# Where the writes of split queries and keys are issued in a two-layer cross-attention kernel

## The chip, the core and the metric

The kernel is written for Trainium2 and runs on one core of one chip. A core has a matrix engine (TensorE, PE in the profile; its weight loads are listed apart as PEld), VectorE (DVE), ScalarE (ACT), GpSimd (POOL) and SyncE (SP), each with an instruction queue of its own that it works through in order. Transfers (DMAs) are issued from the queues of SP, ACT or GpSimd. The metric is the device time of one execution in microseconds. The kernel before takes 3375.44 us, the median of three runs (3371.98 to 3381.5).

## What is computed

Two layers, each of self attention, cross attention against a context of 1601 rows, and a gated feed-forward block, all in 32-bit floats. There are 4 batch elements, 512 positions, width 320, 20 heads of 16, and a hidden width of 1280:

```python
def _attn(x, ctx, wq, wk, wv, wo, bo, heads):
    ...
    q = (x @ wq).reshape(b, n, heads, dh).transpose(0, 2, 1, 3)
    k = (ctx @ wk).reshape(b, j, heads, dh).transpose(0, 2, 1, 3)
    v = (ctx @ wv).reshape(b, j, heads, dh).transpose(0, 2, 1, 3)
    sim = jnp.einsum('bhid,bhjd->bhij', q, k) * scale
    a = jax.nn.softmax(sim, axis=-1)
    out = jnp.einsum('bhij,bhjd->bhid', a, v)
    ...
    return out @ wo + bo
h1 = _ln(x, n1_g, n1_b)
x = _attn(h1, h1, q1, k1, v1, o1_w, o1_b, heads) + x
h2 = _ln(x, n2_g, n2_b)
x = _attn(h2, context, q2, k2, v2, o2_w, o2_b, heads) + x
h3 = _ln(x, n3_g, n3_b)
proj = h3 @ ff_w1 + ff_b1
a, g = jnp.split(proj, 2, axis=-1)
ff = a * jax.nn.gelu(g, approximate=False) @ ff_w2 + ff_b2
return ff + x
```

## The kernel before

Work is cut into units. A unit of attention is one batch element and one group of four heads, so a stage of attention has 4 x 5 = 20 units; a unit of feed-forward is one batch element. In order there are, for each layer, 20 units of self attention, 20 of cross attention and 4 of feed-forward. A unit of attention goes through its keys in chunks of 128 (4 chunks in self attention, 13 in cross attention). The main loop (`main`, from line 1154) does one chunk in two half rounds; the planner's clock (`clock["round"]`) counts half rounds, so a self unit has 8 and a cross unit 26.

In a chunk TensorE forms the scores `st` (L1165): the four heads each use 32 rows of the matrix engine, two products of queries and keys and a third that subtracts the row's maximum, held in `nrows`. ScalarE takes the exponential into `pr` (L1175). TensorE multiplies it with the values into `av` (L1189), ScalarE copies that to `vo` (L1205), and GpSimd adds it onto the unit's output `o` (L1206). `pr` and `vo` share one pool of nine buffers. Beside this, in the same half rounds, TensorE forms the scores `sps` of the next unit (L972), from which VectorE takes the row maxima (L989). At a unit's end these are split, turned and sent to `nrows` by four small transfers (`max_end`, L1050), before the next unit's third products can run.

Queries and keys are held as two parts, high (rounded) and low (the rest), so that a head of 16 fills 32 rows. A projection makes them some units ahead: `both` (L765) for self attention, where queries and keys of one group of heads come in two parts, and `keys_of_context` (L831) and `queries` (L802) for cross attention. ScalarE writes the product to `low` (L781, L810; the keys of context go to `stages` by L840 and L841), then GpSimd splits it: a rounded copy to `high` (L684), and a subtraction that leaves the rest in `low` (L685). `low` and `high` have one buffer each. To bring the parts into the rows that TensorE needs, they are written to `q_way` or `k_way` in DRAM and read back to `q` and `kT` (all at L729). Each of the two ways has two buffers, taken in turn.

These transfers are queued by `move` as entries of `u.moves`, a list for each unit for queries and one for keys. After each step `carry` (L666) issues what is at the head of the lists: an entry may go two half rounds after the one before it in its list (or after the projection), and a call stops once three or more transfers have gone. All go to SP's queue but those of the first unit. A unit has two entries of writes and one of reads. `pending` counts writes not yet issued; a new projection may start when there are none and the reads two users back have been issued (`way_free`). A unit's queries and keys may be used three half rounds after its last reads were issued (`at_hand`, L1401). `at_once` issues at once what a unit that is due still lacks.

When a unit ends, its `o` is divided by the row sums on VectorE and written to `oway` by SP (L1080). After the last group of heads an errand, two half rounds later, reads the batch element's outputs back as `aT` (L1089), and three half rounds after that the output projection (`project`, L1099) may begin, in eight pieces spread between the chunks.

The choice of what runs beside the chunks is made when the program is built: chains of work with a cost and a due time each (`add`, `pick`, `steps`), so the order on every engine is fixed.

Of the kernel before, what the change touches and what calls it, by code (L numbers as in the profile page):

```python
# [65 lines left out]
def kernel(ctx: ExitStack, tc: tile.TileContext, x, context, ws, out):  # L66
# [595 lines left out]
    errands = deque()  # L662
    pending = {"q": 0, "k": 0}
    movers = []

    def carry():  # L666

        room = 3
        for _, what, u in sorted(movers):
            todo = u.moves[what]  # L670
            while todo and todo[0][1]() and clock["round"] >= u.moving[what] + 2 and room > 0:
                room -= todo[0][2]
                todo.popleft()[0]()
            if not todo:
                movers.remove((u.i, what, u))
        while errands and room > 0 and clock["round"] >= errands[0][0] and errands[0][1]():
            errands.popleft()[2]()
# [9 lines left out]
    def add_proj(u):  # L687
# [32 lines left out]

        def move(of, n, pairs, may=None):

            def f():
                if may is None:
                    pending[of] -= 1
                u.moving[of] = clock["round"]
                for i, (to, src) in enumerate(pairs()):
                    queue = (nc.sync, nc.scalar, nc.gpsimd)[i % 3] if start["on"] and u.i == 0 else nc.sync
                    queue.dma_start(out=to, in_=src)  # L729
                if may is not None:  # L730
                    u.open -= 1
                    if not u.open:
                        u.when = -9 if start["on"] else clock["round"]

            if may is None:
                pending[of] += 1
            u.moves[of].append((f, may or yes, n))
            u.moving[of] = clock["round"]
            if (u.i, of, u) not in movers:
                movers.append((u.i, of, u))  # L740

# [5 lines left out]
        def way_free(what):  # L747

            return not pending[what] and (len(users[what]) < 2 or not any(users[what][-2].moves.values()))

        def read_queries(t, keys=None):
# [4 lines left out]

            move("q", 2 if keys is None else 3, pairs, lambda: unread() and (u.cross or free()))

        def both(part):
# [27 lines left out]
            to_q = on_way("q")  # L787
            move("q", 2, lambda: [(to_k[:, 0], high[GD:]), (to_k[:, 1], low[GD:])])
            move("q", 3, lambda: [(to_q[:, e], t[:GD]) for e, t in enumerate((high, low, high))])
            read_queries(to_q, to_k)  # L790
# [4 lines left out]
        def queries():  # L795
# [17 lines left out]
            for i in range(2):  # L813
                rows = slice(i * GD, (i + 1) * GD)
                cols = slice(i * w, (i + 1) * w)
                lo, hi = (t[rows, :w] for t in (low, high))
                pairs = [(to_q[:, e, :, cols], t) for e, t in enumerate((hi, lo, hi))]
                move("q", 3, lambda pairs=pairs: pairs)
            read_queries(to_q)
# [3 lines left out]
        def keys_of_context():  # L823
# [21 lines left out]
            for i in range(2):  # L845
                rows = slice(i * GD, (i + 1) * GD)
                pairs = [(to_k[:, h, :, i], t[rows].rearrange("p a w -> p (a w)")) for h, t in enumerate((high, low))]
                move("k", 2, lambda pairs=pairs: pairs)
            of = to_k.rearrange("j h d i (a w) -> (j h d) i a w", a=4)
# [6 lines left out]

            move("k", 3, reads, free)
            first.made["kv"] += 1
# [193 lines left out]
    def add_finish(u):  # L1052
# [24 lines left out]
        def turn():  # L1077
# [13 lines left out]

            errands.append((clock["round"] + 2, lambda: held["open"] < 2, read))

# [14 lines left out]
        def end(aT):  # L1108
            now = clock["round"]
            held["open"] += 1  # L1110
            for t in range(NQ):
                for part in range(2):
                    add(
                        "project", (0.317,) * 3, lambda t=t, part=part: project(aT, t, part),
                        now + 6 + u.nch * t + u.nch // 2 * part, yes, lambda: clock["round"] >= now + 3,
                    )
# [284 lines left out]
    def at_hand(v):  # L1401

        return v.when is not None and clock["round"] >= v.when + 3

# [159 lines left out]
```

## Time and profile before

| | |
|---|---|
| median of three runs | 3375.44 us |
| the profiled execution | 3384.97 us |
| its span, first to last instruction | 3383.2 us |
| mean granted TensorE clock | 0.946 of full speed |
| ScalarE busy with the exponentials (L1175) | 1407.0 us, 2720 instructions |
| GpSimd busy with the additions onto `o` (L1206) | 741.6 us, 576 instructions |
| transfers | 244.14 MB in 209045 packets |
| of these on SP's and ACT's queue (q1) | 238.02 MB |
| on GpSimd's (q0) | 0.40 MB, three transfers at the start |

A row of the waits reads: who waited (engine, tile, line), who ended the wait, microseconds in all, number of times, the longest. A row of the timeline has the start and the length in microseconds, then the engine (with a q for its queue's own instructions), the line, the operation, out<-in, and in square brackets how long the engine was idle before it and who ended that. A row of the windows has a stretch and its length, then busy microseconds and instructions of each engine, the granted clock, the share of DMA time and GB/s. A row of a group ends with busy microseconds, mean nanoseconds of one, and the idle time before.

### The profile page before, as it was taken

To read this page: it belongs to the slowest core of one execution; us is meant where nothing else is said; L and a number is where in the kernel's file an instruction comes from. 1 tells how busy PE (TensorE), PEld (TensorE's weight loads), DVE (VectorE), ACT (ScalarE), POOL (GpSimd) and SP (SyncE) were. 2 spreads that over 40 slices of the span, in tenths; PEclk is the share of its full clock that TensorE was granted. 3 is DMA by queue.
4 is the path that set the end of the run, shared out by engine and by line. 5 is a ranking of instruction groups with operands and counts; after the bars stand their busy time and mean duration, and the time that the engine had idled before them with its cause. 6 is when DMAs were issued, how large, how long until landed. Compare 5 with 4: busy or idle time off the path is not lost.

```text
span 3383.2 us, 81116 instructions
## 1 busy us (share of the span) xinstructions
PE 3121.4 (92%) x34290; PEld 1649.8 (49%) x34290; DVE 2096.4 (62%) x2819; ACT 1965.6 (58%) x3909; POOL 1130.3 (33%) x1224
## 2 busy tenths in 40 slices
PE   6889889999989989999999888899999899899999
PEld 3445445445545545445554554454454454454555
DVE  3657776767866876732237777667677677675221
ACT  1555656677767777830116665567677677686110
POOL 2333323443434443410113332234344344343000
PEclk7888999999989999999999999899999899999999
DMA  3343322222222222110023332222222122122000
GB/s 90 107 128 123 104 70 80 82 90 63 74 82 64 89 75 64 50 57 1 18 62 120 117 104 88 83 67 72 72 77 77 51 87 72 51 66 77 8 8 16
DMA packets 209045, 244.14 MB, mean 72 GB/s; under 512 B 60412, under 2 KB 140424, under 8 KB 208680
## 3 DMA queue, kind: packets, MB, share of 16 engines
q1 hardware_dynamic: 207924, 238.02, 22.7%
q8 instruction: 269, 4.41, 0.5%
q14 instruction: 96, 0.79, 0.1%
q10 hardware_dynamic: 308, 0.53, 0.1%
q0 software_dynamic: 448, 0.40, 0.0%
HBM read 130.03 MB, written 107.55 MB: 70 GB/s over the span
## 4 chain that ended last, share of the span: by engine, by line
PE 61%; DMA 17%; DVE 8%; SPq 5%; issue 3%; ACT 3%; POOL 1%; ACTq 0%; POOLq 0%; DVEq 0%
PE st L1165 16%; PE av L1189 13%; PE fps L1295 8%; PE yps L1349 5%; DMA q<-qway 4%; DMA qway<-low 4%; DVE pm L989 4%; DMA qway<-high 3%; PE kps L831 3%; SPq L729 3%; PE sps L972 3%; PE ops L1099 3%; ACT pr L1175 2%; DMA aT<-oway 2%; PE fps L1308 2%
## 5 line engine op out<-in xcount | busy, mean ns | idle before, releaser
L1175 ACT ACTIVATE pr<-st 128x512 f32<-128x512 f32 (+1 forms) x2720 | 1407.0, 602 | 449.5 <-PE st L1165 391.0
L989 DVE TENSOR_REDUCE pm<-sps 128x2 f32<-128x1024 f32 (+1 forms) x975 | 1135.5, 1200 | 228.3 <-PE sps L972 192.7
L1206 POOL TENSOR_TENSOR o<-o,vo 128x512 f32<-128x512 f32 x576 | 741.6, 1288 | 1431.3 <-ACT vo L1205 1412.6
L1165 PE MATMUL st<-q,kT 32*128 32x512 f32 (+1 forms) x5120 | 973.8, 448 | 32.6 <-ACT low L781 16.4
L972 PE MATMUL sps<-kT,q 32*128 32x512 f32 x4800 | 883.2, 453 | 97.8 <-DMA q<-qway 75.2
L1189 PE MATMUL av<-pr,vals 128*32 128x512 f32 (+1 forms) x5440 | 774.4, 638 | 27.4 <-ACT pr L1175 21.3
L1165 PEld LDWEIGHTS st<-q,kT 32*128 32x128 f32 (+1 forms) x5120 | 479.0, 186 | 527.4 <-ACT pr L1175 283.3
L1165 PE MATMUL st<-nrows,ones 32*128 32x512 f32 (+1 forms) x2720 | 646.4, 409 | 40.3 <-DMA nrows<-turned 40.2
L989 DVE TENSOR_REDUCE nmax<-sps 128x2 f32<-128x1024 f32 (+1 forms) x343 | 380.1, 1145 | 232.6 <-PE sps L972 179.7
L972 PEld LDWEIGHTS sps<-kT,q 32*128 32x128 f32 x4800 | 386.9, 192 | 152.8 <-DMA q<-qway 45.7
L1205 ACT COPY vo<-av 128x512 f32<-128x512 f32 x576 | 346.9, 602 | 103.7 <-PE av L1189 96.6
L1165 PEld LDWEIGHTS st<-nrows,ones 32*128 32x128 f32 (+1 forms) x2720 | 335.2, 189 | 79.5 <-DMA nrows<-turned 39.2
L1295 PE MATMUL fps<-hT,w 128*128 128x512 f32 x640 | 284.3, 597 | 0.5 <-DVE hid L1319 0.5
L1318 ACT ACTIVATE gl<-fps,b 128x512 f32<-128x512 f32 x80 | 50.7, 684 | 378.0 <-PE fps L1308 272.1
L1189 PEld LDWEIGHTS av<-pr,vals 128*32 128x32 f32 (+1 forms) x5440 | 112.7, 110 | 294.5 <-ACT pr L1175 274.5
L1319 DVE SCALAR_TENSOR_TENSOR hid<-fps,b,gl 128x512 f32<-128x512 f32 x80 | 56.4, 746 | 265.1 <-ACT gl L1318 265.1
L1295 PEld LDWEIGHTS fps<-hT,w 128*128 128x128 f32 x640 | 118.9, 190 | 148.7 <-issue 144.1
L1349 PE MATMUL yps<-w,hid 128*128 128x320 f32 x640 | 175.9, 434 | 0.4 <-ACT hT L529 0.4
L1099 PE MATMUL ops<-wo,aT 112*32 112x160 f32 (+1 forms) x3072 | 139.1, 320 | 27.7 <-DMA aT<-oway 27.4
L1099 PEld LDWEIGHTS ops<-wo,aT 112*32 112x32 f32 (+1 forms) x3072 | 101.3, 118 | 112.7 <-issue 50.7
L1349 PEld LDWEIGHTS yps<-w,hid 128*128 128x128 f32 x640 | 120.5, 190 | 55.7 <-issue 6.6
L781 ACT ACTIVATE low<-qkps,scales 128x256 f32<-128x256 f32 x78 | 35.3, 473 | 157.4 <-PE qkps L765 70.6
(92 smaller groups left out, 2532.5 us busy)
## 6 DMA issues: line engine op xcount, KB each, us to landing
kway<-stages SPq DMA_DIRECT2D x160, 224.0 KB
q<-qway SPq DMA_DIRECT2D x138, 256.0 KB
kT<-kway SPq DMA_DIRECT2D x80, 384.0 KB
oway<-o SPq DMA_DIRECT2D x80, 256.0 KB
kT<-kway SPq DMA_DIRECT2D x40, 256.0 KB
qway<-high SPq DMA_DIRECT2D x160, 64.0 KB
qway<-high SPq DMA_DIRECT2D x79, 128.0 KB
aT<-oway SPq DMA_DIRECT2D x32, 224.0 KB
```

The lines of the kernel that those rows point to most:

```text
L729: queue.dma_start(out=to, in_=src)
L831: nc.tensor.matmul(ps[i * GD : (i + 1) * GD, :w], lhsT=wk_q[rows, k, u.g * GD : (u.g + 1) * GD], rhs=first.kvT[rows, k, i * HALF : i * HAL ...
L972: nc.tensor.matmul(ps, lhsT=u.q[j * SLOT : (j + 1) * SLOT, e, t * P : (t + 1) * P], rhs=u.kT[j * SLOT : (j + 1) * SLOT, u.k0 + s * 512 : u ...
L989: nc.vector.tensor_reduce(to[:, j : j + n], part, AX.X, ALU.max, negate=(ns == 1))
L1099: nc.tensor.matmul(ps[f : f + m, : D // 2], lhsT=aT[:n, k, t * P + f : t * P + f + m], rhs=wo[:n, k, cols], start=(k == 0), stop=(k == 2),)
L1165: nc.tensor.matmul(st[:r, :], lhsT=ones[rows, :r] if e == 2 else u.keys(rows, c), rhs=u.rows[rows, :] if e == 2 else u.q[rows, e, :], star ...
L1175: nc.scalar.activation(p[:r], st[:r], AF.Exp)
L1189: nc.tensor.matmul(ps[j * SLOT : (j + 1) * SLOT, :], lhsT=columns_of[:r, head : head + SLOT], rhs=pr.pop((c, j))[:r, :], start=True, stop= ...
L1205: nc.scalar.copy(vo, ps)
L1206: nc.gpsimd.tensor_tensor(u.o, u.o, vo, ALU.add)
L1295: nc.tensor.matmul(ps, lhsT=w1[:, k, i * FF + c * P : i * FF + (c + 1) * P], rhs=u.hT[:, k, :], start=ahead and k == 0, stop=not ahead and ...
L1349: nc.tensor.matmul(ps[:, :D], lhsT=hid[c][:, t * P : (t + 1) * P], rhs=w2[:, c, :], start=(c == 0), stop=(c == NHC - 1),)
```

## The change

The writes leave the lists. A new function `write` issues them at the place where it is called, which is right behind the split, from GpSimd's queue (those of the first unit stay spread over the three queues). `move` becomes `read` and holds reads alone. `pending` is gone, so a projection no longer waits for the issue of earlier writes. `carry` lets a read go five half rounds after the projection (it was two after the last write); as it runs at every second half round in attention, the reads of most cross units stay six half rounds behind. A unit counts as at hand four half rounds after its last read, not three. The errand that reads `aT` is due four half rounds after the write, not two, and the output projection five after that, not three.

```diff
--- before.py
+++ after.py
@@ -660,7 +660,6 @@
 
     held = {"open": 0, "written": 0, "read": 0}
     errands = deque()
-    pending = {"q": 0, "k": 0}
     movers = []
 
     def carry():
@@ -668,7 +667,7 @@
         room = 3
         for _, what, u in sorted(movers):
             todo = u.moves[what]
-            while todo and todo[0][1]() and clock["round"] >= u.moving[what] + 2 and room > 0:
+            while todo and todo[0][1]() and clock["round"] >= u.moving[what] + 5 and room > 0:
                 room -= todo[0][2]
                 todo.popleft()[0]()
             if not todo:
@@ -718,26 +717,26 @@
         def staged():
             return (one.tile([P, N], F32, tag=n, name=n) for n in ("low", "high"))
 
-        def move(of, n, pairs, may=None):
+        def write(pairs):
+
+            for i, (to, src) in enumerate(pairs):
+                first_one = start["on"] and u.i == 0
+                queue = (nc.sync, nc.scalar, nc.gpsimd)[i % 3] if first_one else nc.gpsimd
+                queue.dma_start(out=to, in_=src)
+
+        def read(of, n, pairs, may):
 
             def f():
-                if may is None:
-                    pending[of] -= 1
-                u.moving[of] = clock["round"]
                 for i, (to, src) in enumerate(pairs()):
                     queue = (nc.sync, nc.scalar, nc.gpsimd)[i % 3] if start["on"] and u.i == 0 else nc.sync
                     queue.dma_start(out=to, in_=src)
-                if may is not None:
-                    u.open -= 1
-                    if not u.open:
-                        u.when = -9 if start["on"] else clock["round"]
-
-            if may is None:
-                pending[of] += 1
-            u.moves[of].append((f, may or yes, n))
+                u.open -= 1
+                if not u.open:
+                    u.when = -9 if start["on"] else clock["round"]
+
+            u.moves[of].append((f, may, n))
             u.moving[of] = clock["round"]
-            if (u.i, of, u) not in movers:
-                movers.append((u.i, of, u))
+            movers.append((u.i, of, u))
 
         def on_way(what):
 
@@ -746,7 +745,7 @@
 
         def way_free(what):
 
-            return not pending[what] and (len(users[what]) < 2 or not any(users[what][-2].moves.values()))
+            return len(users[what]) < 2 or not any(users[what][-2].moves.values())
 
         def read_queries(t, keys=None):
 
@@ -754,7 +753,7 @@
                 reads = [(u.q[:, e].bitcast(F32), by_rows(t[:, e : e + 2])) for e in range(2)]
                 return ([(u.kT[:, u.k0 : u.k0 + N].bitcast(F32), by_rows(keys))] if keys is not None else []) + reads
 
-            move("q", 2 if keys is None else 3, pairs, lambda: unread() and (u.cross or free()))
+            read("q", 2 if keys is None else 3, pairs, lambda: unread() and (u.cross or free()))
 
         def both(part):
 
@@ -785,8 +784,8 @@
                 split(low, high)
             to_k = on_way("k").rearrange("j h d i n -> j h d (i n)")[:, :, :, :N]
             to_q = on_way("q")
-            move("q", 2, lambda: [(to_k[:, 0], high[GD:]), (to_k[:, 1], low[GD:])])
-            move("q", 3, lambda: [(to_q[:, e], t[:GD]) for e, t in enumerate((high, low, high))])
+            write([(to_k[:, 0], high[GD:]), (to_k[:, 1], low[GD:])])
+            write([(to_q[:, e], t[:GD]) for e, t in enumerate((high, low, high))])
             read_queries(to_q, to_k)
             u.keyed = True
             first.made["q"] += 1
@@ -814,8 +813,7 @@
                 rows = slice(i * GD, (i + 1) * GD)
                 cols = slice(i * w, (i + 1) * w)
                 lo, hi = (t[rows, :w] for t in (low, high))
-                pairs = [(to_q[:, e, :, cols], t) for e, t in enumerate((hi, lo, hi))]
-                move("q", 3, lambda pairs=pairs: pairs)
+                write([(to_q[:, e, :, cols], t) for e, t in enumerate((hi, lo, hi))])
             read_queries(to_q)
             u.keyed = True
             first.made["q"] += 1
@@ -844,8 +842,7 @@
             to_k = on_way("k")
             for i in range(2):
                 rows = slice(i * GD, (i + 1) * GD)
-                pairs = [(to_k[:, h, :, i], t[rows].rearrange("p a w -> p (a w)")) for h, t in enumerate((high, low))]
-                move("k", 2, lambda pairs=pairs: pairs)
+                write([(to_k[:, h, :, i], t[rows].rearrange("p a w -> p (a w)")) for h, t in enumerate((high, low))])
             of = to_k.rearrange("j h d i (a w) -> (j h d) i a w", a=4)
 
             def reads():
@@ -854,7 +851,7 @@
                 pairs = [(full[:, :, i * HALF : (i + 1) * HALF], of[:, i, :, :HALF]) for i in range(2)]
                 return pairs + [(to[:, 4 * QT :].rearrange("p (a w) -> p a w", a=4), of[:, 1, :, HALF:])]
 
-            move("k", 3, reads, free)
+            read("k", 3, reads, free)
             first.made["kv"] += 1
 
         def unread():
@@ -1089,7 +1086,7 @@
                     dma(out=aT[:n, k, :], in_=way[at // DH : (at + n) // DH, :DH, :])
                 end(aT)
 
-            errands.append((clock["round"] + 2, lambda: held["open"] < 2, read))
+            errands.append((clock["round"] + 4, lambda: held["open"] < 2, read))
 
         def project(aT, t, part):
             cols = slice(part * D // 2, (part + 1) * D // 2)
@@ -1112,7 +1109,7 @@
                 for part in range(2):
                     add(
                         "project", (0.317,) * 3, lambda t=t, part=part: project(aT, t, part),
-                        now + 6 + u.nch * t + u.nch // 2 * part, yes, lambda: clock["round"] >= now + 3,
+                        now + 6 + u.nch * t + u.nch // 2 * part, yes, lambda: clock["round"] >= now + 5,
                     )
             add("project", 0.0, done, now + 6 + u.nch * NQ)
 
@@ -1400,7 +1397,7 @@
 
     def at_hand(v):
 
-        return v.when is not None and clock["round"] >= v.when + 3
+        return v.when is not None and clock["round"] >= v.when + 4
 
     def at_once(v):
         chain = "early" if v.early else "proj"
```

## The prediction

> **What bounds it now.** I read the page's busy table first, then the table by stage, the waits, and last the timeline around the longest waits.
>
> ```profile
> PE 3121.4 (92%) x34290; PEld 1649.8 (49%) x34290; DVE 2096.4 (62%) x2819; ACT 1965.6 (58%) x3909; POOL 1130.3 (33%) x1224
> ```
>
> TensorE is the bound: 92% of a 3383.2 us span; GpSimd (POOL) is idle two thirds of the time. The table by stage (columns: stretch, its length, busy time of PE, PEld, DVE, ACT, POOL, then granted clock, DMA share, GB/s) holds self attention, cross attention and feed-forward of layer 0, then of layer 1:
>
> ```profile
> 60.00:500.00 440.00, 381.13 (x4196) 209.55 (x4200) 294.27 (x440) 241.65 (x485) 142.27 (x171) 0.89 0.33 105
> 500.00:1420.00 920.00, 855.71 (x11390) 448.24 (x11386) 669.59 (x806) 668.27 (x1344) 380.47 (x348) 0.95 0.24 73
> 1420.00:1760.00 340.00, 337.63 (x1648) 177.11 (x1644) 94.02 (x202) 78.67 (x140) 51.04 (x115) 1.00 0.12 35
> 1760.00:2155.00 395.00, 344.19 (x4081) 192.31 (x4080) 281.82 (x403) 232.14 (x468) 128.84 (x148) 0.93 0.32 104
> 2155.00:3070.00 915.00, 860.24 (x11427) 446.84 (x11421) 663.07 (x767) 672.86 (x1349) 383.62 (x350) 0.95 0.22 68
> 3070.00:3383.00 313.00, 308.70 (x1328) 156.37 (x1326) 74.39 (x157) 64.92 (x113) 29.29 (x71) 1.00 0.10 29
> ```
>
> Feed-forward has no slack: PE full, clock 1.00. The four attention stretches lose twice: PE idles, and the clock is below 1. The clock's share is 0.11 x 440 + 0.05 x 920 + 0.07 x 395 + 0.05 x 915 = 168 us. They hold 320 half rounds of self attention (835 us, 2.6 each) and 1040 of cross attention (1835 us, 1.76 each).
>
> What PE waits for (us in all, times, longest), and one wait of ScalarE:
>
> ```profile
> PE sps L972 <- DMA q<-qway: 75.2, 30, 15.4
> PE st L1165 <- DMA nrows<-turned: 40.2, 12, 5.8
> PE st L1165 <- ACT low L781: 29.7, 12, 4.1
> PE ops L1099 <- DMA aT<-oway: 27.4, 24, 3.0
> PE sps L972 <- DMA kT<-qway: 5.8, 3, 2.6
> ACT low L781 <- DMA qway<-low: 60.5, 14, 6.7
> ```
>
> The 15.4 is the first unit, whose path the change leaves alone: 59.8 + 5.8 = 65.6 us remain for late queries and keys. With nrows, low and aT: 65.6 + 40.2 + 29.7 + 27.4 = 163 us of PE waiting on moves of data. Why they are late shows at two places. First the row of maxima (nrows), then the queries:
>
> ```profile
> 988.16 5.47 SPq L729 DMA_DIRECT2D kway<-stages  x4
> 993.73 4.84 SPq L1050 DMA_DIRECT2D nrows<-turned  x4
> 1003.42 0.79 PE L1165 MATMUL st<-nrows,ones 32*128 32x512 f32 x2 [3.88 <-DMA nrows<-turned]
> 1003.40:1010.20 6.80, 6.78 (x48) 2.85 (x48) 3.16 (x3) 4.30 (x9) 1.28 (x1) 0.53 0.27 67
> ...
> 919.64 0.73 POOL L685 TENSOR_TENSOR low<-low,high 128x256 f32<-128x256 f32 x1
> 923.99 6.57 SPq L729 DMA_DIRECT2D kT<-kway  x3
> 931.20 0.52 SPq L729 DMA_DIRECT2D qway<-high  x1
> 939.18 1.24 SPq L729 DMA_DIRECT2D q<-qway  x2
> 944.92 0.80 PE L972 MATMUL sps<-kT,q 32*128 32x512 f32 x2 [5.88 <-DMA q<-qway]
> 947.89 0.79 PE L972 MATMUL sps<-kT,q 32*128 32x512 f32 x2 [2.17 <-DMA q<-qway]
> 940.50:944.50 4.00, 0.00 (x0) 0.00 (x0) 0.00 (x0) 0.00 (x0) 0.96 (x1) 0.63 0.25 80
> ```
>
> Four key writes went out just ahead of the maxima on the same queue; the maxima, all issued by 998.57, reached PE at 1003.42. After that wait of 3.88 us the clock was 0.53 for 6.8 us: 3.2 us more. In the second place the split was done at 920.4, but SP was held in its three key reads until 930.6 and issued the first query write at 931.20; the reads of 939.18 reached PE at 944.92 and 947.89, 5.7 and 8.7 us on, with a quarter of the DMA engines' time in use (0.25).
>
> **The change, part by part.**
>
> *1. Writes move from SP to GpSimd.* The changed program has 596 of them on GpSimd, five per self unit, four for keys and six for queries per cross unit, each group directly behind its split. SP keeps its reads, maxima, outputs and weights. Its writes cost 0.52 us each to issue (931.20 row), about 310 us of queue time, but what counts is what was queued behind them.
>
> Maxima: the writes ahead of them are gone. I followed the planner's half rounds through both programs (they hold no times): in eleven cross units the maxima came at most two half rounds behind key writes; now no move of SP's stands nearer than four. Taken: 36 of 40.2 us gone; bounds 0 and 40.2.
>
> Queries and keys: in cross attention the read keeps its place, six half rounds behind the projection, but no longer sits behind late writes. In self attention nine units used their queries 3 half rounds after the read; now none has under 4, and 26 have 8. Against it stands the price of a write issued by GpSimd, known from one instance at the start (busy us and mean ns; then KB and us to landing):
>
> ```profile
> L729 POOL DMA_DIRECT2D qway<-high x1 | 0.8, 843 | 0.0
> ...
> qway<-high POOLq DMA_DIRECT2D x1, 128.0 KB, 7.1
> ```
>
> Six query writes need 6 x 0.84 = 5.0 us, and the last lands 7.1 us after its issue begins: 4.2 + 7.1 = 11.3 us after the split, where a read stands about 6 x 1.76 = 10.6 us behind the projection. With projection and split (some 3.5 us) the read issues at about 15 and reaches PE 5.7 us later, at 20.7. Ten cross units use their queries only ten half rounds, 17.6 us, after the projection (sixteen used them at 9 or 11 before): about 3 us each stay, 30 us, and 10 in self attention. Taken: 25 of 65.6 us gone; bounds 65.6 gone, and 20 more than now if all fifteen units at ten or twelve wait long.
>
> *2. GpSimd is held longer.* Queued behind the writes are the o additions, which release the vo buffers. The pool has nine, so the fourth pr two chunks on needs a vo's buffer again:
>
> ```profile
> L1206 POOL TENSOR_TENSOR o<-o,vo x576: 1261/1285/1502, 84.3 to 3076.7; 128x512 f32<-128x512 f32 x192
> ...
> 992.23 0.62 ACT L1205 COPY vo<-av 128x512 f32<-128x512 f32 x1
> 992.95 2.06 ACT L1175 ACTIVATE pr<-st 128x512 f32<-128x512 f32 x4
> 994.98 0.59 ACT L1205 COPY vo<-av 128x512 f32<-128x512 f32 x1
> 995.73 2.05 ACT L1175 ACTIVATE pr<-st 65x512 f32<-65x512 f32 x4 [0.17 <-PE st L1165]
> ...
> 1018.14 0.39 POOL L684 CAST high<-low 128x256 fp32r<-128x256 f32 x1
> 1018.62 0.73 POOL L685 TENSOR_TENSOR low<-low,high 128x256 f32<-128x256 f32 x1
> 1020.28 0.62 ACT L1205 COPY vo<-av 128x512 f32<-128x512 f32 x1
> ```
>
> The vo ended at 992.85; its buffer is needed at 995.73 + 3 x 0.51 = 997.3, 4.4 us later. Less 1.29 for the addition, GpSimd may be 3.1 us late. At the query split it is free at 1019.35 + 5.04 = 1024.4, 3.5 us behind the vo that ended at 1020.90: 0.4 us over. Laid in this way over all 79 splits of the trace, each with its own vo times, the overrun is 12 us at 0.84 us a write, 42 at 1.0, 105 at 1.2 and 229 at 1.5; ScalarE has 0.1 to 0.2 us free between chunks here, so I count it whole. The price comes from one issue, whose shape (64 rows) is that of the others; taken 25 us, between 0.84 and 1.0, bounds 0 (hidden by the same slack) and 105.
>
> [...]
>
> *3. One buffer each for low and high.* ScalarE's write of the next `low` waits until the writes that read the old one have landed; behind it in ScalarE's queue stand the exponentials. Without the old condition on pending writes the next projection of a self unit may start sooner: spacings were mostly 6 or 8 half rounds, now seven are 0 to 2, one 3, eleven 4. The splits of this shape:
>
> ```profile
> L684 POOL CAST high<-low 128x512 fp32r<-128x512 f32 x39 | 23.9, 612 | 221.0 <-ACT low L781 135.5 <-DMA nrows<-turned 22.4 <-ACT pr L1175 22.3
> L685 POOL TENSOR_TENSOR low<-low,high 128x512 f32<-128x512 f32 x39 | 49.8, 1276 | 3.1
> ```
>
> From the end of one projection to a free `low`: 0.6 + 1.3 + 3 x 0.84 + 7.1 = 11.5 us, about 12 with ScalarE's own copy. At 2.2 us a half round (2.6 less the stalls) the waits are 12 at spacing 0, 7.6 at 2, 5.4 at 3, 3.2 at 4: 12 + 6 x 7.6 + 5.4 + 11 x 3.2 = 98 us, against 60.5 now. PE shared half of that (29.7); I take 0.6 of the longer ones, 59 us: 29 us more. Bounds: 0, if landings are shorter, and 100.
>
> *4. Output projection four half rounds later.* 4 x 1.76 = 7 us exceed the longest aT wait, 3.0 us. Taken 25 of 27.4 us gone; bounds 0 and 27.4. The later end of a batch element is covered by the other elements' units.
>
> *5. Sum.* Waits: -36 - 25 + 29 - 25 = -57 us of 163. The clock follows the waits: 168 us lost for 163 waited, 1.03 each, so -59. GpSimd +25. Together -91 us. The profiled execution took 3385.0 us, 1.8 beyond its span and 9.5 above the median of the runs, 3375.4. The median becomes 3284; I say 3285.
>
> **Rivals.**
>
> *Slower: the issue price.* The place is GpSimd's queue behind a split. From about 1.25 us a write the overrun passes the 116 us of gain; at 1.5 us it is 229 - 116, +113: 3490. For: one instance is thin evidence, and six stand back to back. Against: that instance took 0.84 including whatever a first use costs. 17%.
>
> *No change: `low` eats it.* If landings take 10 us under load rather than 7.1, each of the 19 close spacings waits 2.9 us more: 55 on ScalarE, 33 on PE, 67 with the clock; and the queries lose half of their gain, 25 with the clock: -91 + 67 + 25 = +1: 3375. For: DMA share is highest in self attention, 0.33 and 0.32. Against: 7.1 was measured with other writes in flight. 13%.
>
> *It hardly does what it says.* SP still stands at its reads, now waiting for slower landings; only aT (25) and a third of the maxima (12) go: -37 - 38 + 25 = -50: 3325. [...] 11%.
>
> *Much faster.* All 133 us of late queries, keys, maxima and aT go, `low` stays as it is: -133 x 2.03 + 12 = -258: 3117. For: nothing slow would then stand before SP's reads. Against: the 11.3 us above. 9%.
>
> **How the numbers follow.** My forecast, 50%, runs from 3225 to 3350 by the terms' bounds. About 0.3%, 10 us, is what a measurement can tell. Faster: 50 + 11 + 9 and 1 of the no-change case, 71%; same 8%; slower: the issue price and the rest of the no-change case, 21%. The range from 3150 to 3415 leaves out most of the first rival and half of the last.
>
> **What would show it.** SP's waits for GpSimd splits vanish; PE's wait for nrows is under 10 us, for aT under 5, for queries about 40 beside the first unit; ScalarE's wait for `low` about 100 us, in self attention alone; GpSimd busy about 1130 + 596 x 0.84 = 1630 us; clock in cross attention 0.97 or more. The forecast is wrong if ScalarE's pr begins to wait for GpSimd's additions, if a write costs over 1.2 us, or if query waits stay above 60.

## The result, and the profile after

The changed kernel takes 3386.18 us, the median of 20 runs, against 3373.92 for the kernel before in as many: a ratio of 1.004 with an interval of 1.0026 to 1.0053. It is 0.4% slower, where 2.7% faster had been forecast. Timed once more beside the experiments the ratio was 1.0013 (1.0002 to 1.0024).

The first profiled execution of the changed kernel took 3371.36 us, the fastest of its runs, so where a span is compared a second trace of the same kernel is used, whose execution took 3387.93 us. Both tell the same story. The busy line of the first, and the shares of the chain of waits, before (first fence) and after:

```profile
PE 61%; DMA 17%; DVE 8%; SPq 5%; issue 3%; ACT 3%; POOL 1%; ACTq 0%; POOLq 0%; DVEq 0%
```

```profile
PE 3091.2 (92%) x34290; PEld 1633.7 (48%) x34290; DVE 2110.4 (63%) x2823; ACT 1965.0 (58%) x3909; POOL 1492.8 (44%) x1819
...
PE 55%; POOL 14%; issue 11%; DVE 9%; ACT 5%; DMA 5%; SPq 0%; POOLq 0%; ACTq 0%; DVEq 0%
```

Transfers and SP's queue have lost most of their share (17% to 5%, 5% to nothing), and GpSimd has come into the chain (1% to 14%). That is the exchange which the rest is about. The share of issue, time for which the profile names no cause, rose as well (3% to 11%); what lies behind it was not followed. The table by stage, self and cross attention of layer 0:

```profile
60.00:500.00 440.00, 388.91 (x4478) 213.65 (x4480) 307.00 (x455) 258.25 (x518) 221.07 (x293) 0.93 0.39 110
500.00:1420.00 920.00, 848.04 (x11329) 441.52 (x11331) 674.56 (x818) 675.34 (x1358) 485.27 (x530) 0.97 0.28 75
```

The clock rose (0.89 and 0.95 before; layer 1 is alike), but in cross attention PE is busy for 848 us of the stretch, where it was 856: it works faster and waits longer. Timed by the exponentials (320 in each stage of self attention, 1040 in each of cross attention), the two self stages together took 834 us before and take 814 in the second trace, and the two cross stages 1902 and 1917: the change gains in the one and loses in the other. The waits of the first trace:

```profile
PE st L1162 <- ACT vo L1202: 78.4, 57, 5.0
PE st L1162 <- ACT low L780: 51.0, 14, 6.2
PE sps L969 <- DMA q<-qway: 22.5, 5, 15.6
PE st L1162 <- DMA nrows<-turned: 22.2, 8, 4.4
PE vps L893 <- ACT low L780: 7.4, 3, 4.4
...
ACT vo L1202 <- POOL o L1203: 111.8, 70, 5.3
ACT low L780 <- DMA qway<-low: 79.1, 16, 10.2
```

Late queries, keys, maxima and aT made 75.2 + 5.8 + 40.2 + 27.4 = 148.6 us before; now they make 22.5 + 22.2 = 44.7. But the wait for `low` grew from 33.0 (29.7 + 3.3 at the values) to 58.4, and 78.4 us stand in a row that did not exist: PE waits for a `vo` copy, which ScalarE holds back for an addition of GpSimd. The sum is 181.5 us, where it was 181.6. What the moved writes cost GpSimd (busy us, mean ns; then KB and us to landing):

```profile
L725 POOL DMA_DIRECT2D qway<-high x239 | 149.3, 626 | 7.9 <-DMA kway<-stages 4.2 <-issue 2.0 <-DMA nrows<-turned 1.7
L725 POOL DMA_DIRECT2D kway<-stages x160 | 99.6, 628 | 2.8 <-issue 2.8
```

```profile
kway<-stages POOLq DMA_DIRECT2D x160, 224.0 KB, 6.8
qway<-high POOLq DMA_DIRECT2D x160, 64.0 KB, 2.9
qway<-high POOLq DMA_DIRECT2D x79, 128.0 KB, 5.7
```

One write is 0.63 us, cheaper than the 0.84 reckoned with. So it is not the price of a write that failed. A typical place in the timeline of the second trace, GpSimd first, then ScalarE, then TensorE's wait; and the windows before, in and behind that wait:

```profile
574.33 0.93 POOL L683 CAST stages<-stages 128x896 fp32r<-128x896 f32 x1 [1.27 <-ACT stages L838]
575.34 2.11 POOL L684 TENSOR_TENSOR stages<-stages 128x896 f32<-128x896 f32 x1
577.40 2.49 POOL L725 DMA_DIRECT2D kway<-stages  x4
579.90 1.27 POOL L1203 TENSOR_TENSOR o<-o,vo 128x512 f32<-128x512 f32 x1
...
576.29 0.62 ACT L1202 COPY vo<-av 128x512 f32<-128x512 f32 x1
577.02 2.06 ACT L1172 ACTIVATE pr<-st 128x512 f32<-128x512 f32 x4
581.21 0.59 ACT L1202 COPY vo<-av 128x512 f32<-128x512 f32 x1 [2.13 <-POOL o L1203]
...
581.85 0.69 PE L1162 MATMUL st<-q,kT 32*65 32x512 f32 x2 [1.78 <-ACT vo L1202]
```

```profile
574.00:580.00 6.00, 6.00 (x63) 2.51 (x57) 5.90 (x9) 4.64 (x10) 5.57 (x7) 1.00 0.10 12
580.07:581.85 1.78, 0.00 (x1) 0.00 (x2) 1.24 (x2) 0.64 (x2) 1.11 (x1) 0.97 0.81 186
581.73:585.14 3.41, 3.29 (x17) 0.92 (x17) 1.23 (x1) 2.12 (x5) 1.27 (x1) 0.50 0.66 186
```

A key split and its four writes hold GpSimd from 574.33 to 579.89. The `vo` that ended at 576.91 is added from 579.90 to 581.17, and at 581.21 the *next* `vo` begins, after 2.13 us of waiting. It is the next `vo`, not a `pr` two chunks on, that needs the buffer: in the program's table of addresses 498 of the 576 `vo` tiles have the address of the `vo` five tiles earlier. ScalarE was ready at 579.08, so the addition might have been 579.08 - 576.91 - 1.27 = 0.90 us late, not 3.1. PE lost 1.78 us, and then ran 3.41 us at half clock. The kernel before has the same order of buffers, but there only the splits themselves hold GpSimd: no addition began more than 0.6 us after its `vo`, and ScalarE never waited for one.

### The profile page after: what moved, and what is told of

The parts are those of the page before. It is cut to its first block, busy times and chain, and to the rows that moved or that the text cites. A ratio compares the mean times of both kernels' runs of the same rounds, so it can differ in the third digit from the quotient of the medians.

```text
span 3369.6 us, 81232 instructions
## 1 busy us (share of the span) xinstructions
PE 3091.2 (92%) x34290; PEld 1633.7 (48%) x34290; DVE 2110.4 (63%) x2823; ACT 1965.0 (58%) x3909; POOL 1492.8 (44%) x1819
## 4 chain that ended last, share of the span: by engine, by line
PE 55%; POOL 14%; issue 11%; DVE 9%; ACT 5%; DMA 5%; SPq 0%; POOLq 0%; ACTq 0%; DVEq 0%
PE st L1162 15%; PE av L1186 12%; PE fps L1292 8%; PE yps L1346 5%; POOL o L1203 4%; DVE pm L986 4%; ACT pr L1172 3%; POOL qway L725 3%; PE kps L829 3%; PE vps L911 3%; PE ops L1096 2%; POOL kway L725 2%; PE fps L1305 2%; DMA qway<-low 2%; PE sps L969 2%
## 5 line engine op out<-in xcount | busy, mean ns | idle before, releaser
L1162 PE MATMUL st<-q,kT 32*128 32x512 f32 (+1 forms) x5120 | 977.9, 443 | 121.3 <-ACT vo L1202 78.1
L969 PE MATMUL sps<-kT,q 32*128 32x512 f32 x4800 | 864.1, 447 | 43.6 <-DMA q<-qway 22.5
L1186 PE MATMUL av<-pr,vals 128*32 128x512 f32 (+1 forms) x5440 | 764.9, 630 | 34.6 <-ACT pr L1172 29.4
L1162 PE MATMUL st<-nrows,ones 32*128 32x512 f32 (+1 forms) x2720 | 646.2, 404 | 25.5 <-DMA nrows<-turned 22.2
L969 PEld LDWEIGHTS sps<-kT,q 32*128 32x128 f32 x4800 | 376.3, 188 | 92.0 <-DVE pm L986 36.3
L725 POOL DMA_DIRECT2D qway<-high x239 | 149.3, 626 | 7.9 <-DMA kway<-stages 4.2
```

Of the source, the lines that this page charges most:

```text
L969: nc.tensor.matmul(ps, lhsT=u.q[j * SLOT : (j + 1) * SLOT, e, t * P : (t + 1) * P], rhs=u.kT[j * SLOT : (j + 1) * SLOT, u.k0 + s * 512 : u ...
L1162: nc.tensor.matmul(st[:r, :], lhsT=ones[rows, :r] if e == 2 else u.keys(rows, c), rhs=u.rows[rows, :] if e == 2 else u.q[rows, e, :], star ...
L1186: nc.tensor.matmul(ps[j * SLOT : (j + 1) * SLOT, :], lhsT=columns_of[:r, head : head + SLOT], rhs=pr.pop((c, j))[:r, :], start=True, stop= ...
```

## The experiments

Ratios are to the kernel before on the same chip. The median of the kernel before was 3380.56 to 3386.95 us on the four chips of the experiments, and 3373.92 in the runs of the result, so kernels run on different chips are compared by ratio.

**The changed kernel again.**

> The changed kernel itself, timed beside the kernels below and the kernel of before. If the ratio of 1.004 holds here, it is about 13 us above the kernel of before; the kernel without part 4 was at 0.995. Theory (part 4 is worth nothing once the writes are on GpSimd): the ratio is 0.993 to 1.000 here too. Rival (part 4 costs something on top of the moved writes, 10 us or more): 1.002 to 1.006.

3389.43 us against 3383.58, 1.0013 (1.0002 to 1.0024), between the two statements. Its busy line and its waits, in a span of 3386.1 us, are much like those of the first trace:

```profile
PE 3108.3 (92%) x34290; PEld 1638.4 (48%) x34290; DVE 2113.2 (62%) x2823; ACT 1967.2 (58%) x3909; POOL 1493.6 (44%) x1819
```

```profile
PE st L1162 <- ACT vo L1202: 80.2, 56, 5.5
PE st L1162 <- ACT low L780: 52.7, 14, 6.3
PE sps L969 <- DMA q<-qway: 23.0, 5, 16.4
PE st L1162 <- DMA nrows<-turned: 19.1, 6, 4.4
...
ACT vo L1202 <- POOL o L1203: 112.4, 69, 5.8
```

**Buffers of vo in turn.** The changed kernel with nine `pr` and `vo` buffers used strictly one after the other, so that a `vo`'s buffer is wanted nine tiles on, as the prediction had it.

```diff
-    prs = ctx.enter_context(tc.tile_pool(name="prs", bufs=9))
+    nine = [const.tile([P, N], F32, name=f"pr{i}") for i in range(9)]
+    turns = {"n": 0}
+    def pr_tile():
+        turns["n"] += 1
+        return nine[turns["n"] % 9]
...
-                p = prs.tile([P, N], F32, tag="pr", name="pr")
+                p = pr_tile()
...
-                vo = prs.tile([P, N], F32, tag="pr", name="vo")
+                vo = pr_tile()
```

> The changed kernel, with the nine buffers of pr and vo taken strictly in turn, so that a vo's buffer is written again nine tiles later and not by the next vo. Theory (GpSimd's writes hold up the additions that free the one buffer which every vo takes): ScalarE's wait for the additions falls from 111.8 us to under 20, PE's 78 us behind vo are gone, and the time falls by 78 us or more, to 3310 us or less. Rival (the waits behind vo only show where something else would stop PE a little later): the waits for vo go, the waits for pr, low or queries grow by as much, and the time stays between 3370 and 3395 us.

3328.71 us, 0.9842 (0.9823 to 0.986). The same additions, splits and 596 writes stand on GpSimd, and it is busy 1495.8 us; only the buffers' order differs.

```profile
PE st L1169 <- ACT low L787: 55.0, 14, 6.9
PE st L1169 <- DMA nrows<-turned: 31.4, 11, 4.6
...
ACT pr L1179 <- POOL o L1210: 7.2, 5, 3.4
```

ScalarE's wait for GpSimd fell from 112.4 to 7.2 us and PE's row behind `vo` is gone. So the wait is made by which tile takes the buffer next. The time fell by 63 us of span (3386.1 to 3322.8) for 80 us of wait removed, 12 of which came back as later maxima (19.1 to 31.4). That is less than the 78 us or more of the theory, and far outside the rival's range. The two cross stages account for all of it (1917 to 1856 us; self attention 814 and 813), and 76 of PE's 80 us behind `vo` lay in cross attention.

**The same ring in the kernel before.**

> Control: the kernel of before with the ring of nine pr and vo buffers that took 53 us off the changed kernel. Theory (the wait for vo's buffer is made by the moved writes): within 10 us of the kernel of before. Rival (the ring helps whatever issues the writes): 30 us or more below it.

3395.86 us, 1.0028 (1.0016 to 1.004): no gain, and some 10 us longer. The ring pays only where GpSimd issues the writes.

**A tenth buffer.** Its room is that of the second aT buffer; nothing else is changed.

```diff
-    prs = ctx.enter_context(tc.tile_pool(name="prs", bufs=9))
+    prs = ctx.enter_context(tc.tile_pool(name="prs", bufs=10))
...
-                aT = two.tile([P, 3, N], F32, tag="aT", name="aT")
+                aT = one.tile([P, 3, N], F32, tag="aT", name="aT")
...
-            errands.append((clock["round"] + 4, lambda: held["open"] < 2, read))
+            errands.append((clock["round"] + 4, lambda: held["open"] < 1, read))
```

> The changed kernel with a tenth pr and vo buffer in the same pool, its room taken from the second aT buffer. With ten, a vo's buffer is next wanted by a pr eleven tiles on, more than two chunks, which is what the prediction had supposed for nine. Theory (the wait comes from the next vo wanting the same buffer, not from GpSimd's load as such): ScalarE's wait for the additions falls from 111.8 to under 15 us and the time by 40 to 65 us, to a ratio of 0.980 to 0.988. Rival (additions late by more than two chunks, or one aT buffer costs what the tenth gains): 0.992 or more.

3348.57 us, 0.99 (0.9877 to 0.9923), between the two statements, and the expectation's premise was wrong: eleven tiles is the distance from the `pr` that held a `vo`'s buffer before it, not to the tile that takes it next. With ten, a `vo`'s buffer goes to a `pr` six tiles on, not eleven, and the trace shows it:

```profile
549.95 2.62 POOL L1203 TENSOR_TENSOR o<-o,vo 128x512 f32<-128x512 f32 x2
...
545.77 0.62 ACT L1202 COPY vo<-av 128x512 f32<-128x512 f32 x1
...
551.26 2.06 ACT L1172 ACTIVATE pr<-st 128x512 f32<-128x512 f32 x4 [2.17 <-POOL o L1203]
```

The `pr` of 551.26 waits for the first of the two additions, that of the `vo` of 545.77. Four `pr` from 546.54 and a `vo` at 548.47 lie between, so it is the sixth. ScalarE's wait for GpSimd is 61.1 us. Five tiles on it was 112.4, six 61.1, nine 7.2: the wait falls as the slack in tiles grows.

**Two buffers for low and high**, in the changed kernel, with the same change of aT as above.

```diff
-            return (one.tile([P, N], F32, tag=n, name=n) for n in ("low", "high"))
+            return (two.tile([P, N], F32, tag=n, name=n) for n in ("low", "high"))
```

> The changed kernel with two buffers each for low and high; to make room aT has one buffer, and a batch element's outputs are read only when the output projection before is done. Theory (in self attention ScalarE stands behind the landing of the writes): ScalarE's wait for low falls from 79.1 us to under 10, PE's 51.0 us behind low go, nothing changes in cross attention, and the time falls by 50 to 100 us, to between 3285 and 3335 us. Rival (self attention is held by the DMA engines, which are busiest there): the wait moves to the queries, and the time falls by less than 20 us.

3306.15 us, 0.9777 (0.9761 to 0.9793). The rows of PE waiting for `low` are gone, and the others stay:

```profile
PE st L1162 <- ACT vo L1202: 80.5, 55, 6.2
PE st L1162 <- DMA nrows<-turned: 20.1, 6, 4.4
```

59 us of waiting for `low` (52.7 + 6.3) were worth 92 us of span (3386.1 to 3294.5; by the ratios it is about 80). As the theory says, the gain lies in self attention: its two stages fell from 814 to 733 us, those of cross attention stayed (1917 and 1912). What one aT buffer does by itself was not run.

**Both at once.**

> The changed kernel with nine pr and vo buffers strictly in turn, two buffers for low and for high, and one for aT. The ring alone gave -53 us, the double buffers alone -76 us. Theory (two separate waits, at vo and at low): they add, 3245 to 3270 us, with TensorE's waits behind vo and behind low both under 10 us. Rival (one wait hides behind the other, or what is left is the late rows of maxima): 3290 us or more, with waits for nrows or queries grown to take their place.

3244.73 us, 0.9581 (0.9565 to 0.9598). The two add: 0.017 and 0.024 of the ratio alone, 0.043 together. Of the waits for moved data, what is left is the first unit and the maxima:

```profile
PE st L1169 <- DMA nrows<-turned: 37.3, 13, 4.8
PE sps L976 <- DMA q<-qway: 25.6, 6, 15.7
```

**Writes at the same place, on SP's queue.** Right behind the split as in the changed kernel, but issued by SP.

```diff
-                queue = (nc.sync, nc.scalar, nc.gpsimd)[i % 3] if first_one else nc.gpsimd
+                queue = (nc.sync, nc.scalar, nc.gpsimd)[i % 3] if first_one else nc.sync
```

> The changed kernel, with the same writes at the same place in the program but issued by SP. Theory (the engine matters): SP stands at each split until GpSimd has done it, PE's waits for maxima and queries come back to 60 us or more together, the waits for vo go, and the time is about that of before, 3355 to 3390 us. Rival (the place behind the split matters, not the engine that issues): waits for maxima, queries and aT stay as low as in the changed kernel (under 40 us beside the first unit), and without the waits for vo the time is 3320 us or less.

3503.9 us, 1.0355 (1.0334 to 1.0375). SP's waits for the splits, and PE's for the maxima:

```profile
SPq L725 <- POOL high L683: 488.5, 54, 150.0
SPq L725 <- POOL stages L683: 394.0, 38, 19.0
...
PE st L1162 <- DMA nrows<-turned: 184.7, 38, 11.0
```

SP stands at a write until its split is done, and the maxima stand behind it. GpSimd does the split itself: in the first trace of the changed kernel its writes waited 16.3 us in all (8.5 booked as issue, 6.1 for key writes to land, 1.7 for maxima), none of it for a split. The waits went the theory's way, but the time lies 114 us above its range, and the rival is further off still. At this place SP waits 883 us for the splits; in the kernel before, whose lists hold a write back for two half rounds, it was 486. So with SP in GpSimd's place the span is 108 us longer (3494.2 and 3386.1), even without the waits for `vo`; that bears out the reason of part 1, but it is not the price that the writes had in the kernel before.

**Part 4 alone, on the kernel before.** Reads of aT two half rounds later, the output projection two half rounds later still (first lines of the diff); and then the projection's half alone (last lines).

```diff
-            errands.append((clock["round"] + 2, lambda: held["open"] < 2, read))
+            errands.append((clock["round"] + 4, lambda: held["open"] < 2, read))
...
-                        ... yes, lambda: clock["round"] >= now + 3,
+                        ... yes, lambda: clock["round"] >= now + 5,
```

> The kernel before with one part of the change alone: aT is read four half rounds after the write, and the output projection begins five after that. Theory (the waits for aT add to the time, each with its share of the clock): PE's 27.4 us behind aT fall under 5 and the time falls by 25 to 55 us, to between 3320 and 3350 us. Rival (they lie beside other waits): the time moves by less than 10 us.

> The kernel of before with half of part 4: only the output projection's first allowed half round moves from three to five behind the end of the attention, the reads of aT stay where they were. Theory (TensorE waited because the projection came before its rows had landed, and gaps in front of it were booked as issue): most of part 4's -95 us comes with this half, -70 to -100, waits for aT under 10 us. Rival (SP stood at the aT reads and held the maxima and queries behind them, so the later read is what counts): -40 us or less, with waits for queries still above 65 us beside those for aT.

3289.2 us, 0.9727 (0.9712 to 0.9741), and 3294.11 us, 0.9724 (0.9709 to 0.9738). Two half rounds more for the projection bring all of it, as the theory of the second expectation has it; the theory of the first had asked for 3320 to 3350 us, about half the gain. The waits with the projection's half alone:

```profile
PE sps L972 <- DMA q<-qway: 60.9, 24, 15.7
PE st L1165 <- DMA nrows<-turned: 36.7, 12, 6.1
...
PE ops L1099 <- DMA aT<-oway: 4.8, 7, 1.0
```

The wait for aT fell from 27.4 to 4.8 and that for queries from 75.2 to 60.9; the span fell by 91 us. Gaps in front of the output projection that are booked as "issue" shrank too (the weight loads of `ops` waited 50.7 us for issue before, 30.2 now), so the row for aT may understate its wait. In all PE was idle for 40 us less and busy for 51 us less; how much of that belongs to aT was not followed.

**The change without part 4.**

> The change without its part 4: the reads behind the output (aT) and the output projection begin as early as before; writes on GpSimd and reads five half rounds behind stay. Theory (the parts are costs and gains of their own that add): part 4 alone gave -95 us on the kernel of before, the whole change +12, so this should lie about 95 above the changed kernel, 3455 to 3490 us, with some 25 us of TensorE's waits for aT back and ScalarE's wait for vo still near 110 us. Rival (part 4 gains only because it clears SP's queue, which the moved writes have already cleared): within 30 us of the changed kernel, 3365 to 3415 us, with waits for aT under 10 us.

3370.43 us, 0.9952 (0.9934 to 0.997). The rival stands: the parts do not add. Part 4 is worth 95 us on the kernel before, and here it costs 0.6%.

```profile
PE st L1162 <- ACT vo L1202: 64.4, 51, 6.4
...
PE ops L1096 <- DMA aT<-oway: 3.4, 5, 0.8
```

With the writes off SP's queue the wait for aT is 3.4 us without any later projection. Parts 1 and 4 cure the same wait for aT, and part 4 has nothing left to take there. To see what it costs, the same with the ring, and with the ring and the double buffers:

> The changed kernel with the ring of nine pr and vo buffers and without part 4. Without part 4 the changed kernel was 0.6% faster than with it (0.9952 against 1.0013), although TensorE's waits for aT were short in both. Theory (part 4 costs only by where it lays the splits against the vo waits, 64.4 us of TensorE without it and 80.2 with it): with the vo waits gone there is no difference, a ratio of 0.981 to 0.988 like the ring with part 4 (0.9842). Rival (part 4 costs by itself once writes are on GpSimd): 0.974 to 0.980.

> The changed kernel with the ring, two buffers for low and high and one for aT, but without part 4. Theory (with the writes off SP's queue the rows of the output land in time whether or not the projection waits): within 15 us of the same kernel with part 4, a ratio of 0.954 to 0.963. Rival (the waits for vo and low had hidden a late aT): waits for aT of 15 us or more, a ratio of 0.966 or more.

0.9835 (0.9819 to 0.9852) against 0.9842 with part 4, and 0.9579 (0.9562 to 0.9596) against 0.9581. Once the waits for `vo` are gone part 4 makes no difference; its 0.6% in the changed kernel comes with those waits. How it lays the splits against them was not followed.

**Part 4 and double buffers, writes still on SP.**

> The kernel of before with part 4 and two buffers for low and high, writes still on SP. Theory (without the moved writes the wait for low is short, 16.7 us of TensorE and 45.9 of ScalarE, and its end is worth about twice TensorE's share): 3240 to 3265 us. Rival (the wait for low covers lateness of SP's writes, which shows elsewhere once it is gone): 3275 us or more, with waits for queries or nrows grown by 15 us or more.

3280.58 us, 0.9675 (0.9654 to 0.9695): half a per cent under part 4 alone, the rival's time. PE's wait for `low` (16.7 us) went, and queries and maxima took most of it back (14 us together, just under the 15 that the rival asked for):

```profile
PE sps L972 <- DMA q<-qway: 57.4, 20, 16.3
PE st L1165 <- DMA nrows<-turned: 45.2, 18, 5.8
```

They were 52.3 and 35.9 with part 4 alone. That fits a lateness of SP's queue of which `low` had hidden some.

**Reads two half rounds behind the projection instead of five**, in the changed kernel.

```diff
-            while todo and todo[0][1]() and clock["round"] >= u.moving[what] + 5 and room > 0:
+            while todo and todo[0][1]() and clock["round"] >= u.moving[what] + 2 and room > 0:
```

> The changed kernel with its reads two half rounds behind the projection instead of five; the writes stay on GpSimd. Theory (the later read keeps SP from standing before writes that have not landed, with the maxima behind it): SP's waits for landings grow by 100 us or more, TensorE's waits for nrows grow from 19 to 50 us or more, and the time to a ratio of 1.010 or more. Rival (the reads are hidden wherever they stand, so the five half rounds are worth nothing): 0.997 to 1.006, with nrows under 30 us.

3401.13 us, 1.0061 (1.0039 to 1.0083), at the upper edge of the rival's. SP's wait for the key writes to land grew from 248.8 to 367.3 us, but PE's for the maxima only from 19.1 to 29.6, with 6.9 more for keys:

```profile
SPq L732 <- DMA kway<-stages: 367.3, 73, 19.7
...
PE st L1162 <- DMA nrows<-turned: 29.6, 12, 4.1
PE sps L969 <- DMA kT<-kway: 6.9, 2, 4.3
```

The later reads are worth about half a per cent. The queries' row is 23.3 us here too, so the gain there came with the writes' new engine and place, not with the later reads.

## Why the prediction was wrong

Each part against the rows of the second trace:

| step | forecast, us | measured, us |
|---|---|---|
| 1, maxima | -36 | 40.2 to 19.1: -21 |
| 1, queries and keys | -25 | 75.2 + 5.8 to 23.0: -58 |
| 4, aT | -25 | 27.4 to none: -27 |
| 3, `low` | +29 | 33.0 to 59.0: +26 |
| 2, GpSimd held | +25 | none to 80.2 on PE, 112.4 on ScalarE |
| sum without the clock | -32 | 0 |

The step that failed is part 2: "The pool has nine, so the fourth pr two chunks on needs a vo's buffer again", and from it that GpSimd may be 3.1 us late. The pool gave a `vo` the buffer of the `vo` before it, so GpSimd may be 0.9 us late. A key split with its four writes holds it for 5.5 us (0.93 + 2.11 + 2.49) and a query split with its six for 4.9 (0.40 + 0.73 + 6 x 0.62), where the splits alone had held it for 3.0 and 1.1. The 25 us that had been laid became 80.2 on PE. Made true by the ring, the supposition gives the wait that it promised, 7.2 us on ScalarE and none of PE behind `vo`, and the time is then 0.9842 of the kernel before, 53 us less. So some 60 of the 100 us between forecast and result go back to this step.

The reckoning also laid only the 79 splits of `low`, not the 40 of `stages`; of the 72 places where ScalarE waits for an addition in the second trace, 32 have four key writes in the 9 us before them (59 us of waiting) and 31 six query writes (51 us), so about half lay outside it. The price of a write, on which the slower rival was built, was not the cause: at 0.63 us it was below all the prices that had been weighed. It had been called known from one instance, but the trace before holds two more issues of GpSimd, of 704 and 580 ns. No write of GpSimd in the first trace took over 814 ns, and the median was 622. The forecast's own sign of failure was right in kind, ScalarE waiting for GpSimd's additions, and named `pr` (4.7 us) where it was `vo`.

Part 1 was right in its mechanism: SP's waits for the splits vanished, and the kernel with SP as issuer shows what they can cost. SP did stand longer for writes to land, as the rival "It hardly does what it says" had it (110.9 us before, 208.0 now for the queries' low parts), but PE's waits for queries fell all the same. They gained twice the forecast, 6.6 us beside the first unit instead of 40, and the 64 KB writes of cross attention landed after 2.9 us, where 7.1 had been laid. The maxima kept 19 us instead of 4, and 31 and 37 in the kernels with the ring. Lateness of SP does not explain these: ahead of each of the six waits in the second trace SP issued the first of the four transfers within 0.1 us of the end of `turned`, where at four of the twelve places before it was 3.4 to 8.4 us behind. Why they are late was not followed. Part 3 was right in mechanism and size (ScalarE's wait for `low` was 83 us in the second trace, 98 had been laid). A small slip is in the half rounds: the stretch from 500 to 1420 us leaves out the end of its cross stage, which by the exponentials took 1.83 us a half round, not 1.76; it shortens the query waits as laid by a few us.

Part 4 was right in sign for the kernel before and undersized: 25 us with the clock's share of 26 were booked, and 95 were measured there. But in the sum it was wrong to book it beside part 1, which alone takes the aT wait to 3.4 us.

The clock term, 1.03 us for each us waited, does not hold as one price for every wait. Below are PE's waits for queries, keys, maxima, `low`, aT and `vo` added up, PE's idle time (span less busy), the span and the clock of most of the traces:

| kernel | these waits, us | PE idle, us | span, us | clock |
|---|---|---|---|---|
| writes on SP behind the split | 272.0 | 369.3 | 3494.2 | 0.941 |
| before | 181.6 | 261.8 | 3383.2 | 0.946 |
| changed, second trace | 181.3 | 277.8 | 3386.1 | 0.956 |
| changed, without part 4 | 162.0 | 270.7 | 3364.4 | 0.960 |
| before, later projection alone | 139.0 | 221.5 | 3292.1 | 0.962 |
| changed, two `low` | 125.1 | 226.7 | 3294.5 | 0.969 |
| before, part 4 alone | 121.3 | 211.2 | 3286.7 | 0.963 |
| changed, ring | 120.3 | 230.9 | 3322.8 | 0.964 |
| changed, ring and two `low` | 65.1 | 185.4 | 3244.3 | 0.975 |

From first to last 250 us of span go with 207 us of these waits, 1.2 us for each, where 2.03 had been used, but the kernels do not lie on one line: part 4 alone and the ring have nearly the same sum and differ by 36 us. The table also answers why the result is a tie: the change exchanged some 106 us of waits for as many others. That the clock rose from 0.946 to 0.956 brought 13 us of PE's busy time (3121.4 to 3108.3), but PE's idle time rose by 16 (261.8 to 277.8). By kind, a us of waiting behind `vo` cost about 1.0 (ring: 63 us of span for 61 less of the sum), one behind `low` 1.6 (92 for 56), and the kernel with the later projection alone fell by 91 us for 43 less of the sum.

Between the kernel before and the ring the price of the clock itself is not what failed. There these waits fell by 61 us, about the 57 of the forecast, but PE's idle time by only 31, since other waits grew (that of the values for `pr` from 21.3 to 33.6); and with those 31 us PE's busy time fell by 30 (3121.4 to 3091.9), close to the 1.03. So the forecast also failed in taking waits that go as waits that stay gone. With the writes on SP the price does not hold either way: idle time 108 us above that of the kernel before, busy time 3.5. What decides it was not followed. Nor had the 25 us of GpSimd been given a share of the clock, though a wait for `vo` can cost clock, as at 581.85 above.

## What to carry to other kernels

A buffer's slack is read from who takes it next in the built program, not from the number of buffers: with the same nine buffers ScalarE's wait for the additions was 112 us in one order and 7 in another. When issues are moved to an engine that also releases buffers, lay out every stretch in which it is held, each kind of split included, against that slack. And when two edits cure the same wait, run each alone before adding them: here one was worth 95 us alone and cost 0.6% beside the other.

## What the runs showed of the hardware that was not expected

The granted clock has only two values in the trace before and the first trace of the changed kernel, 1.00 and 0.50, and the half comes in pieces of 3.41 us (of the 52 half-clock stretches before, 28 are two pieces long and 13 are one; of the 46 after, 24 are one; only a trace's last stretch, 3.16 us before and 3.32 after, is a part of one). In the second trace the wait of 1.78 us at 580.07, with PE busy through the 6 us ahead of it, was followed by 3.41 us at 0.50. Not every wait was: in the first trace PE was busy through the 6 us ahead of 1209.92 and then stood still for 2.58 us, and the clock was 1.00 through them and the 6.8 us behind.

Writes on GpSimd waited for older writes to land. In the first trace of the changed kernel the last query write behind a split stood for 1.62 us behind key writes still in flight, and with it the addition and, for 5.31 us, ScalarE:

```profile
1142.07 0.62 POOL L725 DMA_DIRECT2D qway<-high  x1 [1.62 <-DMA kway<-stages]
1142.70 1.27 POOL L1203 TENSOR_TENSOR o<-o,vo 128x512 f32<-128x512 f32 x1
...
1144.01 0.58 ACT L1202 COPY vo<-av 128x512 f32<-128x512 f32 x1 [5.31 <-POOL o L1203]
```

All such waits of that trace together are some 6 us on GpSimd (4.2 in the row of query writes above, 1.9 in that of the low parts), so they lengthen a few places and do not carry the result.
